# A ternary-expert transformer block on one core: the first block's attention worked by halves of its tokens, with its norms interleaved

## The chip, the core and the metric

The kernel runs on one core of one Trainium2 chip. The metric is the device time of one launch in microseconds (us). Below, PE is TensorE, DVE is VectorE, ACT is ScalarE, POOL is GpSimd and SP is the engine that issues the DMAs. PSUM is the memory that matmuls accumulate in.

## What is computed

4096 tokens of width 512 pass an attention over 64 fixed latent keys per head (16 heads of 32, the best four keys of each head count), and then a gated feed-forward layer whose three weight matrices are rounded to {-1, 0, 1} times one scale. Cut to what matters:

```python
Q = (h @ Wq.T + bq) by heads;  V = (h @ Wv.T + bv) by heads      # h = layernorm(x)
attn_logits = einsum('bhtd,lhd->bhtl', Q, latent) / sqrt(HD)
topk_logits, topk_idx = top_k(attn_logits, 4)
weighted = softmax(topk_logits) times the selected latents
x = x + layernorm((weighted + V) @ Wo.T + bo)
wu, wg, wd = ternary_quant(W_up), ternary_quant(W_gate), ternary_quant(W_down)
# ternary_quant(w): scale = mean(|w|) + 1e-8; clip(round(w / scale), -1, 1) * scale
g = layernorm(x)
x = x + layernorm((silu(g @ wu.T) * (g @ wg.T)) @ wd.T)
```

## The kernel before

The tokens are worked in eight blocks of 512, each of four tiles of 128 rows. A block's feed-forward layer is cut into 16 chunks of 128 hidden columns, called experts in the code. In the loop over the blocks (L687) the expert loop of block b carries the attention of block b+1 in pieces, placed by hand (`pieces`, L617: `put(e, k, f)` runs step f at place k of expert e). Only block 0's attention has no expert loop to hide in. It is written out ahead of the loop (L467 to L592), beside the preparation of the weights. The kernel uses a manual schedule: every engine carries out its instructions in the order in which the code issues them, and semaphores keep the data right.

The steps of an attention (class `Attention`, L211) are:

- `a_stats`, `a_rstd`, `a_apply`, `a_trans`: layer norm of a tile of x (statistics on DVE, the root on POOL in L190 and L191, the application on DVE) and its transposition by PE into `hT`, copied out of PSUM by ACT or DVE (L241, L243).
- `q(c)`: four matmuls of 128x512 into PSUM (L250), and ACT adds the bias (L255). c is one of four chunks of 128 columns, which hold four heads.
- `l(c)`: the logits of the chunk, in two PSUM tiles, one for each pair of heads, over all 512 tokens (L264); ACT scales them into two tiles w (L272). Such a pair is an "item" of 128 x 8 x 64 numbers, and there are eight items, i = 2c and 2c+1.
- `m(i)`, `r(i)`, `n(i)` on DVE: the eight largest of each row of 64 (L282), marking of the best four (L290), subtraction of the best (L292), and, after the exponentials `e(i)` on ACT (L299, L300), sum, reciprocal, mask and scaling (L305 to L310).
- `t(c)`: PE transposes two items (L322), ACT copies them to `wT` (L325). `v(c)`: the values, four matmuls (L334). `y(c)`: the weighted latents are added to the values in the same PSUM tile (L342), and ACT writes `attnT` with the bias (L346).
- `o(t, chunks)`: the output projection of token tile t (L355), accumulated over the four chunks. Before the loop, the four tiles' sums lie in four PSUM tiles (`acc_psum`) from the first chunk to the last.
- `o_bias`, `o_rstd`, `o_apply`: DVE adds the bias (L362) and takes statistics, POOL the root, DVE normalises (L196), and POOL or DVE adds to x (L371).
- `f_stats`, `f_rstd`, `f_apply`, `f_trans`: the second norm, the transposition (L206), and a split into two operands `hT_f` (ACT, L392) and `lT_f` (DVE, L393), which the experts' matmuls read.

An expert makes `pu` and `pg` (L409), DVE and ACT combine them to hidden columns, and `down` (L445) of the expert before adds its part to four PSUM tiles with the signs of the third matrix.

Each weight matrix (u, g, d) arrives in four chunks of 128x2048. `sum_abs` on ACT (L151, about 2 us) adds up the absolute values; `scale` adds the four sums over the partitions by a small matmul `tot` on PE (L155) and makes the scale and its inverse on DVE; `rounded` (L167, POOL, about 2 us) rounds a chunk, and `sign` (L171, ACT, about 2 us) makes the ternary chunk `tern`. The u and g chunks are prepared between the items of block 0's attention. Of d, two sums are taken at the end of that stage, and `down_weights` (L595) places the rest in the first experts: the two last sums and the scale in expert 0, the first sign in expert 1, the others in experts 2 to 4.

What limits the order around the change: `ps_at` holds two PSUM tiles that q, l, t, tot and all transpositions take in turn; `ps_up` holds two more (tags u and g), which v takes before the loop and pu and pg in it; `ps_acc` holds four.

Of the kernel before, what the change touches and what calls it, by code (L numbers as in the profile page):

```python
# [16 lines left out]
P = 128  # L17
# [15 lines left out]
def latent_attention_ternary_glu(  # L33
# [49 lines left out]
    x_tiles = {}  # L83

# [67 lines left out]

    def scale(n):
# [21 lines left out]
    class Norm:  # L175
        def __init__(self, name):
            self.name = name
            self.mv = small.tile([P, TT, 2], F32, tag="mv", name=f"mv_{name}")
            self.rs = small.tile([P, TT], F32, tag="rs", name=f"rs_{name}")

# [5 lines left out]
        def rstd(self, lo, hi, scale=None):  # L186
# [5 lines left out]
            if scale is not None:  # L192
                nc.gpsimd.tensor_scalar(rs, rs, scale[0], 0.0, ALU.mult, ALU.add)

# [16 lines left out]
    class Attention:  # L211
# [90 lines left out]
        def n(self, i):  # L302
            w = self.w[i]
            ri = small.tile([P, G], F32, tag="ri", name=f"ri_{self.b}_{i}")
# [92 lines left out]

    class Experts:
# [68 lines left out]
    A = Attention(0, hT_0, attnT_0)  # L467
# [4 lines left out]
    for t in range(TT):  # L472
        A.a_apply(t)
        A.a_trans(t, nc.vector if t % 2 else nc.scalar)
    nxt = Attention(1)

    def values(c):
        A.v(c, lambda name: ps_up.tile([P, 512], F32, tag="ug"[c % 2], name=name))

    def output(c):  # L480
        A.y(c)
        for t in range(TT):
            A.o(t, [c], acc_psum)

    sum_abs("u", 0)
# [3 lines left out]
    sum_abs("u", 2)  # L491
    A.q(1)

    A.m(0)
    A.r(0)
    A.e(0)

    sum_abs("u", 3)
    A.l(1)
    A.m(1)  # L500
    A.n(0)
    A.r(1)
    A.e(1)
# [4 lines left out]
    for k in range(DC):  # L508
        rounded("u", k, nc.gpsimd)

    A.q(2)
    values(0)
    sum_abs("g", 0)
    A.m(2)
    A.n(1)
    A.r(2)
    A.t(0)
    A.e(2)

    A.l(2)  # L520
    output(0)
    sum_abs("g", 1)
    A.m(3)
    A.n(2)
    A.r(3)
    A.e(3)

    A.q(3)
    values(1)
    sum_abs("g", 2)  # L530
    A.m(4)
    A.n(3)
    A.r(4)
    A.t(1)
    A.e(4)

    A.l(3)
    output(1)
    sum_abs("g", 3)
    A.m(5)  # L540
    A.n(4)
    A.r(5)
    A.e(5)
    scale("g")
    for k in range(DC):
        rounded("g", k, nc.gpsimd)

    values(2)
    sign("u", 0)
    A.m(6)  # L550
    A.n(5)
    A.r(6)
    A.t(2)
    A.e(6)

    output(2)
    values(3)
    sign("u", 1)
    sign("u", 2)
    A.m(7)  # L560
    A.n(6)
    A.r(7)
    A.e(7)

    sign("u", 3)
    A.n(7)
    A.t(3)
    output(3)
    for k in range(DC):
        sign("g", k)  # L570
    sum_abs("d", 0)
    sum_abs("d", 1)
    for t in range(TT):
        nxt.a_stats(t)
    nxt.a_rstd(0, 4)
    A.o_bias(0)
    A.o_bias(1)
    A.o_rstd(0, 2)
    A.o_bias(2)
    A.o_bias(3)  # L580
    A.o_rstd(2, 4)
    for t in range(TT):
# [209 lines left out]
```

## Time and profile before

| what | value |
|---|---|
| time before, median of 3 runs | 1259.86 us (1256.70 to 1261.38) |
| time of the profiled execution | 1260.48 us |
| its span in the profile | 1258.7 us |
| first value matmul (pv) of block 0 | 37.59 us |
| last output projection of block 0 begins | 84.84 us, for 3.70 us |
| last step n of block 0's items ends on DVE | about 80.4 us |
| HBM traffic over the span | 24.91 MB read, 8.39 MB written, 26 GB/s |

The page gives for each engine its busy time, then the busy share in 40 slices, then groups of instructions. Most of what matters here lies in the first three to four slices of 31.5 us each, so the page's averages say little of it; the busy time by stretch and the instructions in order of time do. In the latter, each row has start, duration, engine, line and operation, and in brackets how long the engine was idle before it and which instruction released it. "x8" for four f32 matmuls of q counts two passes of each. The DMA engines are busy from 2 to about 52 us with the weights and the first two blocks of x, and hardly at all afterwards:

```profile
25.00:40.00 15.00, 12.28 (x37) 5.82 (x36) 14.54 (x79) 7.65 (x13) 7.29 (x4) 0.77 1.02 404
40.00:55.00 15.00, 13.97 (x53) 6.82 (x52) 11.40 (x72) 8.48 (x15) 1.86 (x1) 1.00 0.88 323
55.00:70.00 15.00, 12.62 (x54) 6.31 (x52) 9.20 (x38) 8.99 (x15) 4.58 (x3) 1.00 0.00 1
```

The columns are the stretch and its length, then busy time and number of instructions of PE, weight load, DVE, ACT and POOL, then the granted TensorE clock as a share of full speed, the DMA share and GB/s.

### The profile page before, as it was taken

The numbers are of one execution on the slowest core, as the hardware profiler recorded it, in microseconds if no ns is written. First come the engines' busy times: TensorE is split into PE (matmuls) and PEld (weight loads), VectorE is DVE, ScalarE is ACT, GpSimd is POOL, SyncE is SP. The second block draws the span as 40 slices with busy tenths as digits, with TensorE's granted clock in tenths as the row PEclk, the third lists the DMA queues.
The fourth block names the chain that finished last, engine by engine and source line by source line (L and its number), as shares of the span: only waits on it lengthen the run. The fifth ranks groups of instructions, "written<-read, shape, count | busy, mean of one in ns | idle before, by whom it ended". The sixth has DMA issues, their size and how long they took to land.

```text
span 1258.7 us, 14275 instructions
## 1 busy us (share of the span) xinstructions
PE 1205.8 (96%) x4998; PEld 817.1 (65%) x4998; DVE 796.4 (63%) x2834; ACT 399.3 (32%) x675; POOL 174.2 (14%) x196
## 2 busy tenths in 40 slices
PE   5966999999999999999999999999999999999996
PEld 3424666676767666686675766666666767657884
DVE  4785575576747667485764767566684767737334
ACT  4574533133322333133331333213332233312221
POOL 0243000320003200032002210032000320013102
PEclk9996999999999999999999999999999999999998
DMA  9600000010000100001000010001000000000000
GB/s 366 260 1 0 1 1 1 0 36 33 1 1 1 68 1 1 1 1 67 1 1 1 1 68 1 1 1 67 1 2 0 1 35 1 1 1 1 34 1 34
DMA packets 14712, 34.21 MB, mean 27 GB/s; under 512 B 1456, under 2 KB 1456, under 8 KB 13616
## 3 DMA queue, kind: packets, MB, share of 16 engines
q1 hardware_dynamic: 14640, 33.30, 7.2%
q8 instruction: 39, 0.64, 0.2%
q14 instruction: 33, 0.27, 0.1%
HBM read 24.91 MB, written 8.39 MB: 26 GB/s over the span
## 4 chain that ended last, share of the span: by engine, by line
PE 89%; DVE 1%; POOL 1%; ACT 0%; issue 0%; POOLq 0%; ACTq 0%
PE pg L409 19%; PE acc L445 19%; PE pu L409 19%; PE pq L250 8%; PE po L355 8%; PE pv L334 8%; PE pv L342 2%; PE pw L322 2%; PE pl L264 2%; PE pt_f L206 1%; PE pt_a L206 1%; DVE h L426 0%; DVE y L196 0%; POOL x L460 0%; POOL rs_y L191 0%; ACT junk_high L151 0%
## 5 line engine op out<-in xcount | busy, mean ns | idle before, releaser
L409 PE MATMUL pg<-hT_f,tern_g 128*128 128x512 f32 x512 | 220.6, 431 | 0.0
L445 PE MATMUL acc<-tern_d,hi 128*128 128x512 f32 x512 | 213.5, 417 | 4.1 <-DVE y L196 4.1
L409 PE MATMUL pu<-hT_f,tern_u 128*128 128x512 f32 x512 | 210.2, 411 | 0.7 <-ACT hT_f L392 0.7
L426 DVE TENSOR_TENSOR h<-h,pg 128x512 f32<-128x512 f32 x128 | 87.3, 682 | 192.0 <-PE pg L409 191.2
L409 PE MATMUL pu<-lT_f,tern_u 128*128 128x512 f32 x512 | 204.0, 399 | 0.0
L409 PE MATMUL pg<-lT_f,tern_g 128*128 128x512 f32 x512 | 202.3, 395 | 0.0
L445 PE MATMUL acc<-tern_d,lo 128*128 128x512 f32 x512 | 202.1, 395 | 0.1
L418 ACT ACTIVATE h<-pu,half_u 128x512 f32<-128x512 f32 x128 | 87.7, 685 | 231.2 <-PE pu L409 230.1
L430 ACT CAST hi<-h 128x512 fp32r<-128x512 f32 x128 | 79.4, 621 | 253.9 <-DVE h L426 253.6
L421 DVE SCALAR_TENSOR_TENSOR h<-h,pu 128x512 f32<-128x512 f32 x128 | 87.0, 680 | 108.2 <-ACT h L418 108.2
L409 PEld LDWEIGHTS pg<-hT_f,tern_g 128*128 128x128 f32 x512 | 96.6, 189 | 51.4 <-issue 18.1
L250 PE MATMUL pq<-hT,wq 128*128 128x512 f32 x256 | 122.1, 622 | 1.5 <-issue 0.8
L445 PEld LDWEIGHTS acc<-tern_d,hi 128*128 128x128 f32 x512 | 96.4, 188 | 39.1 <-DVE y L196 12.2
L355 PE MATMUL po<-wo,attnT 128*128 128x512 f32 x256 | 115.5, 593 | 3.8 <-ACT attnT L346 3.8
L409 PEld LDWEIGHTS pg<-lT_f,tern_g 128*128 128x128 f32 x512 | 96.6, 189 | 28.5 <-issue 8.4
L334 PE MATMUL pv<-hT,wv 128*128 128x512 f32 x256 | 115.1, 592 | 0.0
L409 PEld LDWEIGHTS pu<-hT_f,tern_u 128*128 128x128 f32 x512 | 97.3, 190 | 24.1 <-issue 1.7
L409 PEld LDWEIGHTS pu<-lT_f,tern_u 128*128 128x128 f32 x512 | 97.3, 190 | 23.3 <-issue 1.7
L445 PEld LDWEIGHTS acc<-tern_d,lo 128*128 128x128 f32 x512 | 96.6, 189 | 22.8 <-issue 3.3
L435 DVE TENSOR_TENSOR lo<-h,hi 128x512 fp32r<-128x512 f32 x128 | 91.5, 715 | 21.9 <-ACT hi L430 21.9
L190 POOL TENSOR_SCALAR rs_o<-mv_o 128x2 f32<-128x2 f32 x16 | 5.7, 354 | 707.0 <-DVE mv_o L184 707.0
L290 DVE MATCH_REPLACE8 left<-m,w 128x64 f32<-128x64 f32 x512 | 100.4, 209 | 0.0
(101 smaller groups left out, 1336.1 us busy)
## 6 DMA issues: line engine op xcount, KB each, us to landing
x<-in_x SPq DMA_DIRECT2D x32, 256.0 KB, 4.0
out_x<-x SPq DMA_DIRECT2D x32, 256.0 KB, 2.0
raw_u<-in_wuT SPq DMA_DIRECT2D x4, 1024.0 KB, 11.8
raw_g<-in_wgT SPq DMA_DIRECT2D x4, 1024.0 KB, 16.6
raw_d<-in_wdT SPq DMA_DIRECT2D x4, 1024.0 KB, 16.2
wq<-in_wqT SPq DMA_DIRECT2D x1, 1024.0 KB, 7.5
wv<-in_wvT SPq DMA_DIRECT2D x1, 1024.0 KB, 16.7
wo<-in_woT SPq DMA_DIRECT2D x1, 1024.0 KB, 17.0
```

The costliest lines, as they stand in the source:

```text
L206: nc.tensor.transpose(pt[:, c * P : (c + 1) * P], h[:, c * P : (c + 1) * P], ident)
L250: nc.tensor.matmul(pq, lhsT=wq[:, k, c * P : (c + 1) * P], rhs=self.hT[:, k, :], start=(k == 0), stop=(k == DC - 1),)
L290: nc.vector.match_replace(left[:, g, :], m8[:, g, :], w[:, g, :], TAKEN)
L334: nc.tensor.matmul(self.pv[c], lhsT=wv[:, k, c * P : (c + 1) * P], rhs=self.hT[:, k, :], start=(k == 0), stop=False,)
L355: nc.tensor.matmul(self.po[t], lhsT=self.attnT[:, c, t * P : (t + 1) * P], rhs=wo[:, c, :], start=(c == 0), stop=(c == DC - 1),)
L409: nc.tensor.matmul(p, lhsT=tern[n][k][:, e * P : (e + 1) * P], rhs=part[:, k, :], start=(k == 0 and i == 0), stop=(k == DC - 1 and i == 1),)
L418: nc.scalar.activation(self.h[e], self.pu[e], AF.Tanh, scale=half_u[0])
L421: nc.vector.scalar_tensor_tensor(self.h[e], self.h[e], 1.0, self.pu.pop(e), ALU.add, ALU.mult)
L426: nc.vector.tensor_tensor(self.h[e], self.h[e], self.pg.pop(e), ALU.mult)
L430: nc.scalar.copy(hi, self.h[e])
L435: nc.vector.tensor_tensor(lo, self.h.pop(e), self.hid[e][0].bitcast(F32), ALU.subtract)
L445: nc.tensor.matmul(self.acc[t], lhsT=part[:, t * P : (t + 1) * P], rhs=wd, start=(e == 0 and i == 0), stop=(e == EC - 1 and i == 1),)
```

## The change

Block 0 gets a class of its own, `FirstAttention`. An item is now one chunk of four heads over one half of the tokens (256), instead of one pair of heads over all 512; item i is chunk i % 4 of half i // 4, and it is again 128 x 8 x 64 numbers, so m, r, e and n stay as they are. `l(c)` makes the items c and c+4, each through two PSUM tiles of which half is filled; items 4 to 7 lie in four buffers of the x tiles, which are free at that time. `t`, `v`, `y` and `o` go by item and work on 256 tokens. The bias of the output projection is put into PSUM by a matmul of one row (`o_begin`) ahead of the accumulation; the norm's statistics are taken from PSUM, and ACT applies it (`apply_scalar`, with a shift made by DVE). The order ahead of the loop is written anew: the norms of tiles 0 and 1 (o_stats to f_apply) stand between items 5 and 7, those of tiles 2 and 3 at the end. Two of the sums of u are taken by DVE. All four transpositions of the first norm are copied by ACT. The signs of g move to the end of the stage, the four sums of d into experts 0 and 1, the scale, the rounding and the first sign of d from expert 0 and the start of expert 1 to the middle of expert 1 ("high", just ahead of the first `down`). Of block 1's attention, `q(0)` moves from (1, 0) to (0, 2) and `q(1)` from (2, 0) to (1, 1).

In the two parts that write the order anew (-464 and -507), the removed lines are left out here (they are L464 to L592 above), and so are blank lines and some unchanged ones.

```diff
--- before.py
+++ after.py
@@ -81,6 +81,9 @@
     x_tiles = {}
+    w_later = [
+        work.tile([P, G, L], F32, tag="x", name=f"w_0_{4 + c}", bufs=3 * TT) for c in range(DC)
+    ]
     def load_x(b):
         x_tiles[b] = []
@@ -150,6 +153,11 @@
     def sum_abs(n, c, values=junk):
         nc.scalar.activation(values, raw[n][c], AF.Abs, accum_out=sums[n][:, c : c + 1])
+    def sum_abs_vector(n, c):
+        nc.vector.tensor_reduce(
+            sums[n][:, c : c + 1], raw[n][c], AX.X, ALU.add, apply_absolute_value=True
+        )
     def scale(n):
         tot = at_psum(f"tot_{n}")
         nc.tensor.matmul(tot[:, :DC], lhsT=ones, rhs=sums[n], start=True, stop=True)
@@ -177,6 +185,7 @@
             self.name = name
             self.mv = small.tile([P, TT, 2], F32, tag="mv", name=f"mv_{name}")
             self.rs = small.tile([P, TT], F32, tag="rs", name=f"rs_{name}")
+            self.nm = None
         def stats(self, t, src):
             st = small.tile([P, 6], F32, tag="st", name=f"st_{self.name}_{t}")
@@ -191,6 +200,20 @@
             nc.gpsimd.tensor_tensor(rs, rs, minus_half[:, : hi - lo], ALU.pow)
             if scale is not None:
                 nc.gpsimd.tensor_scalar(rs, rs, scale[0], 0.0, ALU.mult, ALU.add)
+        def shift(self, lo, hi):
+            if self.nm is None:
+                self.nm = small.tile([P, TT], F32, tag="nm", name=f"nm_{self.name}", bufs=1)
+            nc.vector.scalar_tensor_tensor(
+                self.nm[:, lo:hi], self.mv[:, lo:hi, 0], -1.0, self.rs[:, lo:hi],
+                ALU.mult, ALU.mult,
+            )
+        def apply_scalar(self, dst, src, t):
+            nc.scalar.activation(
+                dst, src, AF.Identity, bias=self.nm[:, t : t + 1], scale=self.rs[:, t : t + 1]
+            )
         def apply(self, dst, src, t):
             nc.vector.tensor_scalar(
@@ -301,7 +324,7 @@
         def n(self, i):
             w = self.w[i]
-            ri = small.tile([P, G], F32, tag="ri", name=f"ri_{self.b}_{i}")
+            ri = small.tile([P, G], F32, tag="ri", name=f"ri_{self.b}_{i}", bufs=2)
             nc.vector.tensor_reduce(ri, self.top.pop(i), AX.X, ALU.add)
             nc.vector.reciprocal(ri, ri)
             nc.vector.scalar_tensor_tensor(
@@ -395,6 +418,100 @@
             )
+    class FirstAttention(Attention):
+        HT = TB // 2
+        def l(self, c):
+            qT = self.qT.pop(c)
+            for th in range(2):
+                i = DC * th + c
+                if th == 0:
+                    self.w[i] = work.tile([P, G, L], F32, tag="w", name=f"w_0_{i}", bufs=4)
+                else:
+                    self.w[i] = w_later[c]
+                pls = [at_psum(f"pl_0_{i}_{pr}") for pr in range(2)]
+                for t in range(2):
+                    for pr in range(2):
+                        rows = slice(pr * HP, (pr + 1) * HP)
+                        tokens = slice((2 * th + t) * P, (2 * th + t + 1) * P)
+                        nc.tensor.matmul(
+                            pls[pr][:, t * P : (t + 1) * P],
+                            lhsT=qT[rows, tokens], rhs=lk[rows, c, :],
+                            start=True, stop=True, tile_position=(pr * HP, 0),
+                        )
+                for pr in range(2):
+                    nc.scalar.activation(
+                        self.w[i][:, pr * 4 : pr * 4 + 4, :],
+                        pls[pr][:, : self.HT].rearrange("p (g l) -> p g l", l=L), AF.Copy,
+                        scale=1.0 / math.sqrt(HD),
+                    )
+        def t(self, i):
+            w = self.w.pop(i)
+            self.wT[i] = work.tile([P, 2, TB], F32, tag="wT", name=f"wT_0_{i}", bufs=1)
+            pw = at_psum(f"pw_0_{i}")
+            for g in range(0, G, 2):
+                nc.tensor.transpose(pw[:, g * L : (g + 2) * L], w[:, g : g + 2, :], ident)
+            nc.scalar.copy(
+                self.wT[i][:, :, : self.HT], pw.rearrange("p (r k) -> p r k", k=self.HT)
+            )
+        def tokens(self, i):
+            return slice((i // DC) * self.HT, (i // DC + 1) * self.HT)
+        def v(self, i):
+            c = i % DC
+            self.pv[i] = ps_up.tile([P, TB], F32, tag="ug"[i % 2], name=f"pv_0_{i}")
+            for k in range(DC):
+                nc.tensor.matmul(
+                    self.pv[i][:, : self.HT], lhsT=wv[:, k, c * P : (c + 1) * P],
+                    rhs=self.hT[:, k, self.tokens(i)], start=(k == 0), stop=False,
+                )
+        def y(self, i):
+            c = i % DC
+            pv, wT = self.pv.pop(i), self.wT.pop(i)
+            for pr in range(2):
+                nc.tensor.matmul(
+                    pv[pr * HP : (pr + 1) * HP, : self.HT], lhsT=lv[:, 2 * c + pr, :],
+                    rhs=wT[:, pr, : self.HT], start=False, stop=True, tile_position=(0, pr * HP),
+                )
+            nc.scalar.activation(
+                self.attnT[:, c, self.tokens(i)], pv[:, : self.HT], AF.Identity,
+                bias=bqv_sb[:, 1, c : c + 1],
+            )
+        def o_begin(self, t):
+            self.po[t] = acc_psum(f"po_0_{t}")
+            nc.tensor.matmul(
+                self.po[t], lhsT=ones[0:1, :], rhs=bo_sb[0:1, :], start=True, stop=False
+            )
+        def o(self, i):
+            c = i % DC
+            for t in range(2 * (i // DC), 2 * (i // DC) + 2):
+                nc.tensor.matmul(
+                    self.po[t], lhsT=self.attnT[:, c, t * P : (t + 1) * P], rhs=wo[:, c, :],
+                    start=False, stop=(c == DC - 1),
+                )
+        def o_stats(self, t):
+            self.norm_o.stats(t, self.po[t])
+        def o_rstd(self, lo, hi):
+            self.norm_o.rstd(lo, hi)
+        def o_apply(self, t):
+            o = self.rows["o", t] = row(f"o_0_{t}")
+            self.norm_o.apply_scalar(o, self.po.pop(t), t)
+        def o_add(self, t):
+            nc.vector.tensor_tensor(self.x[t], self.x[t], self.rows.pop(("o", t)), ALU.add)
     class Experts:
         def __init__(self, b, parts):
             self.b = b
@@ -464,42 +581,36 @@
...
+    A = FirstAttention(0, hT_0, attnT_0)
     for t in range(TT):
         A.a_stats(t)
             A.a_rstd(t - 1, t + 1)
     for t in range(TT):
         A.a_apply(t)
+    for t in range(TT):
+        A.a_trans(t)
+    sum_abs_vector("u", 0)
     sum_abs("u", 1)
     A.q(0)
     A.l(0)
+    sum_abs_vector("u", 2)
     A.q(1)
+    sum_abs("u", 3)
     A.m(0)
     A.r(0)
+    A.l(1)
     A.e(0)
+    A.q(2)
     A.m(1)
     A.n(0)
     A.r(1)
+    A.l(2)
     A.e(1)
     scale("u")
@@ -507,96 +618,132 @@
...
     for k in range(DC):
         rounded("u", k, nc.gpsimd)
+    A.q(3)
     A.m(2)
     A.n(1)
     A.r(2)
+    A.l(3)
+    A.v(0)
     A.t(0)
     A.e(2)
+    sum_abs("g", 0)
+    A.y(0)
     A.m(3)
     A.n(2)
     A.r(3)
+    A.v(1)
+    A.t(1)
+    A.y(1)
     A.e(3)
+    sum_abs("g", 1)
+    for t in range(2):
+        A.o_begin(t)
+    A.o(0)
+    A.v(2)
+    A.t(2)
+    A.y(2)
+    A.o(1)
     A.m(4)
     A.n(3)
+    A.v(3)
+    A.t(3)
     A.r(4)
+    A.y(3)
     A.e(4)
+    sum_abs("g", 2)
+    sign("u", 0)
+    A.o(2)
+    A.o(3)
     A.m(5)
     A.n(4)
     A.r(5)
+    A.v(4)
+    A.t(4)
     A.e(5)
+    A.y(4)
+    sum_abs("g", 3)
+    sign("u", 1)
+    for t in range(2):
+        A.o_stats(t)
+    A.o_rstd(0, 2)
+    for t in range(2, 4):
+        A.o_begin(t)
+    A.o(4)
+    A.m(6)
+    A.n(5)
+    A.norm_o.shift(0, 2)
+    A.o_apply(0)
+    A.o_apply(1)
+    A.r(6)
+    A.v(5)
+    A.t(5)
+    A.y(5)
+    A.e(6)
+    sign("u", 2)
     scale("g")
     for k in range(DC):
         rounded("g", k, nc.gpsimd)
+    A.o(5)
+    for t in range(2):
+        A.o_add(t)
+        A.f_stats(t)
+    A.f_rstd(0, 2)
     A.m(7)
     A.n(6)
+    A.v(6)
+    A.t(6)
     A.r(7)
+    A.y(6)
     A.e(7)
     sign("u", 3)
+    A.o(6)
+    A.v(7)
+    for t in range(2):
+        A.f_apply(t)
     A.n(7)
+    A.t(7)
+    A.y(7)
+    A.o(7)
+    sign("g", 0)
+    A.f_alloc()
+    nxt.a_stats(0)
+    nxt.a_stats(1)
+    for t in range(2):
+        A.f_trans(t)
+    for t in range(2, 4):
+        A.o_stats(t)
+        A.o_rstd(t, t + 1)
+    sign("g", 1)
+    nxt.a_stats(2)
+    for t in range(2, 4):
+        A.norm_o.shift(t, t + 1)
+        A.o_apply(t)
+    for t in range(2, 4):
+        A.o_add(t)
+        A.f_stats(t)
+        A.f_rstd(t, t + 1)
+    sign("g", 2)
+    nxt.a_stats(3)
+    for t in range(2, 4):
         A.f_apply(t)
+    for t in range(2, 4):
         A.f_trans(t)
+    sign("g", 3)
     def down_weights(e, place):
+        if (e, place) in ((0, "tanh"), (0, "high"), (0, "down"), (1, "tanh")):
+            c = ((0, "tanh"), (0, "high"), (0, "down"), (1, "tanh")).index((e, place))
+            sum_abs("d", c, work.tile([P, CH], BF16, tag="wT", name=f"junk_d_{c}", bufs=1))
+        elif (e, place) == (1, "high"):
             scale("d")
@@ -606,7 +753,6 @@
             out_scale.extend((first, square))
             for k in range(DC):
                 rounded("d", k, nc.gpsimd)
-        elif (e, place) == (1, "up"):
             sign("d", 0)
         elif e in (2, 3, 4) and place == "gate":
             sign("d", e - 1)
@@ -629,9 +775,10 @@
         put(0, 1, A.a_apply, 3)
         put(0, 2, A.a_trans, 2)
         put(0, 2, A.a_trans, 3)
-        put(1, 0, A.q, 0)
+        put(*((0, 2) if A.b == 1 else (1, 0)), A.q, 0)
         put(1, 1, A.l, 0)
-        put(2, 0, A.q, 1)
+        put(*((1, 1) if A.b == 1 else (2, 0)), A.q, 1)
         put(2, 2, A.l, 1)
         put(3, 0, A.q, 2)
         put(4, 0, A.q, 3)
```

More of the change, by code (lines that the diff above doesn't have):

```diff
@@ L466, in latent_attention_ternary_glu @@
     out_scale = []
-    A = Attention(0, hT_0, attnT_0)
+    A = FirstAttention(0, hT_0, attnT_0)
     for t in range(TT):
@@ L473, in latent_attention_ternary_glu @@
         A.a_apply(t)
-        A.a_trans(t, nc.vector if t % 2 else nc.scalar)
+    for t in range(TT):
+        A.a_trans(t)
     nxt = Attention(1)
[L477 to L487, printed above, removed]
+    sum_abs_vector("u", 0)
     sum_abs("u", 1)
@@ L490, in latent_attention_ternary_glu @@
     A.l(0)
-    sum_abs("u", 2)
+    sum_abs_vector("u", 2)
     A.q(1)
+    sum_abs("u", 3)
     A.m(0)
     A.r(0)
+    A.l(1)
     A.e(0)
-    sum_abs("u", 3)
-    A.l(1)
+    A.q(2)
     A.m(1)
@@ L509, in latent_attention_ternary_glu @@
         rounded("u", k, nc.gpsimd)
-    A.q(2)
-    values(0)
-    sum_abs("g", 0)
+    A.q(3)
     A.m(2)
@@ L516, in latent_attention_ternary_glu @@
     A.r(2)
+    A.l(3)
+    A.v(0)
     A.t(0)
     A.e(2)
-    A.l(2)
-    output(0)
-    sum_abs("g", 1)
+    sum_abs("g", 0)
+    A.y(0)
     A.m(3)
@@ L525, in latent_attention_ternary_glu @@
     A.r(3)
+    A.v(1)
+    A.t(1)
+    A.y(1)
     A.e(3)
-    A.q(3)
-    values(1)
-    sum_abs("g", 2)
+    sum_abs("g", 1)
[6 more added lines that the diff above has]
+    A.o(1)
     A.m(4)
     A.n(3)
+    A.v(3)
+    A.t(3)
     A.r(4)
-    A.t(1)
+    A.y(3)
     A.e(4)
-    A.l(3)
-    output(1)
-    sum_abs("g", 3)
+    sum_abs("g", 2)
+    sign("u", 0)
+    A.o(2)
+    A.o(3)
     A.m(5)
@@ L546, in latent_attention_ternary_glu @@
         rounded("g", k, nc.gpsimd)
[L548 to L559, printed above, removed]
+    A.o(5)
[3 more added lines that the diff above has]
+    A.f_rstd(0, 2)
     A.m(7)
     A.n(6)
+    A.v(6)
+    A.t(6)
     A.r(7)
+    A.y(6)
     A.e(7)
     sign("u", 3)
+    A.o(6)
+    A.v(7)
+    for t in range(2):
+        A.f_apply(t)
     A.n(7)
[L567 to L574, printed above, removed]
-    nxt.a_rstd(0, 4)
[L576 to L582, printed above, removed]
-        A.o_apply(t, nc.vector if t % 2 else nc.gpsimd)
-    for t in range(TT):
-        A.f_stats(t)
-        if t % 2:
-            A.f_rstd(t - 1, t + 1)
-    A.f_alloc()
-    for t in range(TT):
+    A.t(7)
[21 more added lines that the diff above has]
+    nxt.a_stats(3)
+    nxt.a_rstd(0, 4)
+    for t in range(2, 4):
         A.f_apply(t)
-    for t in range(TT):
+    for t in range(2, 4):
         A.f_trans(t)
+    sign("g", 3)
     def down_weights(e, place):
-        if (e, place) in ((0, "tanh"), (0, "high")):
-            values = work.tile([P, CH], BF16, tag="wT", name=f"junk_{place}", bufs=1)
-            sum_abs("d", 2 + (place == "high"), values)
-        elif (e, place) == (0, "down"):
+        if (e, place) in ((0, "tanh"), (0, "high"), (0, "down"), (1, "tanh")):
+            c = ((0, "tanh"), (0, "high"), (0, "down"), (1, "tanh")).index((e, place))
+            sum_abs("d", c, work.tile([P, CH], BF16, tag="wT", name=f"junk_d_{c}", bufs=1))
+        elif (e, place) == (1, "high"):
             scale("d")
```

## The prediction

> **What bounds the kernel now.** I read the page's busy shares and slices first, then the busy time by stretch, then the queues of the first 130 us in order of time.
>
> ```profile
> PE 1205.8 (96%) x4998; PEld 817.1 (65%) x4998; DVE 796.4 (63%) x2834; ACT 399.3 (32%) x675; POOL 174.2 (14%) x196
> ...
> PE   5966999999999999999999999999999999999996
> ```
>
> TensorE is full from slice 5 to slice 39. What changes ahead of that shifts everything behind it; gains there need an earlier start or fewer gaps.
>
> ```profile
> 70.00:85.00 15.00, 12.13 (x37) 5.23 (x38) 12.82 (x62) 10.42 (x13) 5.75 (x4) 1.00 0.01 1
> 85.00:100.00 15.00, 3.54 (x8) 1.28 (x8) 13.55 (x25) 11.58 (x8) 5.83 (x9) 0.72 0.00 1
> 100.00:115.00 15.00, 12.28 (x46) 9.42 (x47) 8.29 (x16) 6.29 (x10) 1.31 (x3) 0.60 0.00 0
> 115.00:130.00 15.00, 12.76 (x55) 8.38 (x54) 4.83 (x9) 7.94 (x11) 8.27 (x4) 0.89 0.00 1
> 130.00:145.00 15.00, 15.00 (x64) 9.64 (x63) 8.79 (x45) 6.31 (x9) 0.00 (x0) 1.00 0.00 0
> ```
>
> The columns are PE, weight load, DVE, ACT, POOL, granted clock, DMA. From 85 to 100 us DVE works through the norms of four tiles while PE does 3.5 of 15 us; afterwards PE runs at a reduced clock. From 130 us on PE has no gap.
>
> ```profile
> 31.18 6.57 PE L250 MATMUL pq<-hT,wq 128*128 128x512 f32 x8
> ...
> 84.84 3.70 PE L355 MATMUL po<-wo,attnT 128*128 128x512 f32 x8 [0.78 <-ACT attnT L346]
> 101.14 1.94 PE L206 MATMUL pt_f<-ident,h_f 128*128 128x128 f32 x8 [12.59 <-DVE h_f L196]
> ...
> 106.34 0.79 PE L409 MATMUL pu<-hT_f,tern_u 128*128 128x512 f32 x1 [0.68 <-ACT hT_f L392]
> ...
> 117.65 0.38 PE L155 MATMUL tot_d<-sums_d,ones 128*128 128x4 f32 x2 [2.24 <-ACT hT L243]
> ...
> 127.94 0.50 PE L445 MATMUL acc<-tern_d,hi 128*128 128x512 f32 x1
> ```
>
> Two marks follow: S, the first expert matmul (pu), at 106.34; and the end of the first down product at 129.89 (the next pu starts there), S+23.55. The down product waits for nothing, since tern_d_0 is made in 125.68 to 127.68 on ACT, from a rounding that began at 118.78 on POOL.
>
> **What the Trainium skill says.** "TensorE: Matmul & The Clock Gate", Part 1: an idle PE falls to half rate and a window of about 3.4 us decides. The trace agrees: clock 0.50 from 31 to 37 us, and the same four-matmul q takes 6.57 us there and 3.43 to 3.70 warm. "GPSIMD Engine Reference", Key points: GpSimd shares SBUF interfaces with VectorE, against instructions with two SBUF inputs. The trace agrees:
>
> ```profile
> 35.27 2.35 DVE L310 TENSOR_TENSOR w<-w,ri 128x512 f32<-128x512 f32 x1
> ...
> 44.14 0.69 DVE L310 TENSOR_TENSOR w<-w,ri 128x512 f32<-128x512 f32 x1
> ```
>
> The first lies beside the rounding, the second does not; a whole step n takes 3.85 instead of 1.58 us, r only 2.48 instead of 2.39. "Perfetto Trace Analysis", Tensor Engine Instruction: ACT and DVE are strictly in order, PE only pulls weight loads ahead. Agrees: pu of expert 1 stood behind the waiting tot_d at 117.65. "VectorE: DVE Perf Modes", tier table: tensor_reduce has only the 1x rate; 2048 elements at that page's 0.96 GHz are an estimated 2.1 us, which no row here shows.
>
> DVE's two longest waits between items, which other work could fill:
>
> ```profile
> 58.01 0.19 DVE L305 TENSOR_REDUCE ri<-top 128x8 f32<-128x32 f32 x1 [4.40 <-ACT top L299]
> ...
> 64.71 0.16 DVE L157 TENSOR_REDUCE total_g<-tot_g 128x1 f32<-128x4 f32 x1 [2.31 <-PE tot_g L155]
> ```
>
> **Unit costs, from the queues in order of time.** DVE per item: m 1.18, n 1.58, r 2.39. PE warm: a 128x512 f32 matmul 0.86, so v on 256 tokens 1.72 and one o item (two matmuls) 1.72; four transposes 0.52; y half of 1.08. ACT: sum_abs 2.02, sign 2.07, wT, attnT and w about 0.4 to 0.6, the exp pair 0.65. Work that halves its tokens I price by half plus the fixed part.
>
> **The change before S, walked queue by queue (us).**
> - Start. All four hT copies go to ACT and DVE's h_a is no longer behind copies: hT complete at 12.4 against 13.8. q0 12.4 to 19.1 (cold, 6.68). The two DVE sums (4.3 together) lie in DVE's old wait of 9.39 before the first MAX8: cost nothing; if that cover failed, m0 would start up to 2 later.
> - Items. A pair item came two to a q; now each q gives one early item and one for the second half, so the first four items need all four q. Each l also fills and empties the two PSUM buffers twice, and the next q waits for that: w_0 at 21.3, q1 22.35 to 26.05; on ACT the sum of raw_u_3 (2.02) stands ahead of w_1, so w_1 only at 29.5. q2 30.45 to 37.0 if cold as at 31.18, q3 40.55 to 44.2, pl_7 done 46.9.
> - DVE meanwhile: m0 21.3, r0 done 25.0, waits for w_1 until 29.5; n0, r1 done 35.1; then total_u waits until 40.55, because tot_u stands on PE behind q2 and both pl of chunk 2. Behind that wait stand m2 and n1, and POOL's rounding of u. n1 costs 3.85; r2 done 48.6, r3 54.15, m5 60.5.
> - From 46.9 PE is its own bound. Per item v 1.72, t 0.52, wait for wT 0.65, y 0.54, o 1.72; plus four new bias matmuls of 0.86. That puts t(3) at 64.8, e(4) at 67.0 (ACT has wT_3 and attnT_3 ahead of it), so DVE waits 6.5 from 60.5. v(6) ends at 83.8.
> - tot_g (79.8) now sits behind y(5). DVE then has scale (0.5), two adds to x beside POOL's rounding of g (2.35 each as in the row above; 0.69 if uncovered), two f_stats (0.8 each), m7 (1.2) and n6 (about 2.4, partly beside rounding): done 90.4. PE idles 83.8 to 90.4 and goes cold.
> - The tail. t6, y6, o6, v7, t7, y7, o7 with their ACT hops, part cold: 12.3, to 102.7. First half's f_trans and lT_f 2.5 (105.2): DVE has these ahead of the second half's o_stats. Then o_stats x2 1.6, POOL's second rstd 1.1 (0.19+0.71 and hops), shift 0.15, the two ACT applies to 109.1, add and f_stats one after the other to 111.4, rstd 1.0, f_apply 0.8, transpose cold 1.5, copy 0.7: S = 115.4.
> The old tail, from the end of n7 (80.35) to S, was 26.0. The first half's norms do leave it (two o_bias and o_stats 3.1, add and apply 2.6, f_stats 1.6, f_apply 0.5: 7.8), but o is not finished sooner: po was complete at 88.5 before, and is at 102.7 now.
> Bounds: the new q0 starts 1.4 earlier in the clock's windows, so q2 may be warm (-3.1, and -1.1 from q0); adds uncovered -3.3; late stretch warm -2. Low end 115.4-9.5 = 105.9, so -0.4; high end +2 for hops I left out, +11. The likeliest takes half the clock's 4.2: S = 113.3, **+7.0**.
>
> **The change after S.** q of block 1, chunk 0, moves ahead of expert 1's pu, into the old wait for hT; q0 cannot start before hT_3 (S+11.8) and pu_1 not before q0. Ends: S+18.8 against S+18.65, no gain. ACT now has all four d sums there (two stood at 92.87 to 96.8, in the old tail), so w_0 comes at S+22.85; q1, pulled forward, waits 1.05 for it (two PSUM buffers) and ends S+26.35. Then tot_d, scale 0.5, one rounding 2.07, one sign 2.0 lie between tot_d and the first down product, which needs tern_d_0: it starts at S+31.25, ends S+33.1. PE stands still 4.65; nothing may pass it. Without the moved q1 (3.43) that is 29.7 against 23.55: +6.1. A pause over one window leaves PE at half rate once more, as at 119 us, where 3.4 us of work took double: +1.7 (between 0 and +3). Together **+7.8** (6 to 9). Later experts: rounding of d runs ahead of their signs; no cost. SP's order of DMAs is unchanged; w_later takes x buffers that block 2's loads need only at expert 4, long after t(7). The DVE accumulations that o_bias made are on PE, the applies on ACT, both counted above.
>
> Sum: 1258.7 + 7.0 + 7.8 = 1273.5 span; the profiled run is 1.8 above its span and 0.6 above the median: 1273.5 + 1.2 = **1274.7**.
>
> **Rivals.**
> 1. The tail's saving meets the new wait and they cancel: items end at 80 as before, S = 106.3-7.8 = 98.5, after S +7.8: 1260. For it: 12.59 us of PE idle stands there to be taken. Against: po complete 14 us later in my walk.
> 2. Ends on the other side: DVE's item chain closes up, its waits (4.40, 2.31 and smaller) filled by norm work. Bound by DVE: 21.3 + 8x5.15 + 11.5 (two scales 1, norms 5.9, contention 4.6) = 74, tail 20 as I walk it: S = 94, so -12.3; after S +6: 1253.5. It decides once items end before about 74.5, which needs total_u, e(4) and tot_g without waits; PE's 39.7 us of work after 46.9 speaks against.
> 3. Slower still: every cold stretch happens and hops add up: +11 +9, 1280.
>
> **Chances.** Forecast with its bounds (1266 to 1278) 0.66, rival 3 0.18, rival 1 0.09, rival 2 0.07. A measurement of this kernel can tell about 0.5% (6.3 us) from no change. Faster 0.07, same 0.09, slower 0.84. The range 1264 to 1282 leaves out rival 2, most of rival 1 and the end of rival 3.
>
> **What would show it.** Right: pu's first matmul at 109 to 116; DVE waiting for PE tot_u about 5 us and for exp of item 4 about 6; PE waiting for DVE before t(6); the first acc waiting 4 to 5 us for ACT's tern_d. Wrong: pu before 104, or no wait at the first acc.

## The result, and the profile after

The changed kernel takes 1279.03 us (median of 4 runs, 1278.40 to 1280.23), the kernel before 1259.16 us (4 runs, 1256.70 to 1261.38). The ratio is 1.0174, with a 95% interval of 1.0156 to 1.0191: slower by 1.7%. The profiled execution took 1280.23 us, with a span of 1278.5 us, 19.8 more than before (1258.7).

The busy shares and slices of the changed kernel:

```profile
PE 1213.8 (95%) x5054; PEld 825.9 (65%) x5054; DVE 796.1 (62%) x2831; ACT 400.0 (31%) x689; POOL 172.3 (13%) x198
...
PE   5866799999999999999999999999999999999996
```

TensorE is full from slice 6 on, one slice later than before. The loss lies ahead of that, so the stretches from 85 to 130 us come next (same columns as before: length, PE, weight load, DVE, ACT, POOL, clock, DMA share, GB/s):

```profile
85.00:100.00 15.00, 7.27 (x22) 3.72 (x21) 14.07 (x45) 4.54 (x6) 9.14 (x6) 0.66 0.06 17
100.00:115.00 15.00, 6.19 (x30) 3.76 (x28) 7.15 (x17) 9.26 (x9) 2.37 (x6) 0.84 0.06 17
115.00:130.00 15.00, 10.12 (x40) 7.63 (x40) 7.26 (x15) 9.50 (x13) 2.40 (x5) 0.70 0.00 1
```

Before, one stretch of 15 us was poor in PE work (85 to 100). Now there are two (85 to 115), and the one from 115 to 130 has 10.1 us of PE where it had 12.8. From 85 to 100 DVE is busy for 14.07 us and POOL for 9.14: they work side by side, while PE waits. The marks on PE, in order of time:

```profile
55.78 3.58 PE L496 MATMUL po<-wo,attnT 128*128 128x512 f32 x4
...
80.93 0.60 PE L456 MATMUL pw<-ident,w 128*128 128x128 f32 x4
...
85.31 1.89 PE L468 MATMUL pv<-hT,wv 128*128 128x256 f32 x8
93.63 1.08 PE L456 MATMUL pw<-ident,w 128*128 128x128 f32 x4 [6.43 <-DVE w L333]
...
104.64 1.98 PE L496 MATMUL po<-wo,attnT 128*128 128x512 f32 x4 [0.57 <-ACT attnT L481]
106.46 1.04 PE L229 MATMUL pt_f<-ident,h_f 128*128 128x128 f32 x8
116.83 1.94 PE L229 MATMUL pt_f<-ident,h_f 128*128 128x128 f32 x8 [9.34 <-DVE h_f L219]
119.45 0.79 PE L526 MATMUL pu<-hT_f,tern_u 128*128 128x512 f32 x1 [0.68 <-ACT hT_f L415]
...
150.24 0.79 PE L562 MATMUL acc<-tern_d,hi 128*128 128x512 f32 x1 [4.81 <-ACT tern_d L179]
```

S, the first expert matmul, stands at 119.45 instead of 106.34 (+13.1). The wait of 12.59 us ahead of the norm's transposes is only 9.34 long now, but a new one of 6.43 stands before item 6's transposes, and the last output projection ends 18 us later than before (106.5 against 88.5). The row at 80.93 is item 5's transposes, from which the experiments below measure. Behind S the down product waits 4.81 us for the first sign of d. By the spans the part behind S costs 19.8 - 13.1 = 6.7 us.

What PE waits for at 93.63 is on DVE. Its queue ahead of that:

```profile
68.79 0.22 ACT L322 ACTIVATE top<-top 128x32 f32<-128x32 f32 x1
```

```profile
69.04 0.18 DVE L328 TENSOR_REDUCE ri<-top 128x8 f32<-128x32 f32 x1 [8.79 <-ACT top L322]
...
83.27 0.16 DVE L165 TENSOR_REDUCE total_g<-tot_g 128x1 f32<-128x4 f32 x1 [3.09 <-PE tot_g L163]
...
83.73 0.67 DVE L512 TENSOR_TENSOR x<-x,o 128x512 f32<-128x512 f32 x1
...
85.27 1.51 DVE L512 TENSOR_TENSOR x<-x,o 128x512 f32<-128x512 f32 x1
...
89.10 2.00 DVE L330 SCALAR_TENSOR_TENSOR w<-left,w 128x512 f32<-128x512 f32 x1
91.14 2.34 DVE L333 TENSOR_TENSOR w<-w,ri 128x512 f32<-128x512 f32 x1
```

```profile
83.97 8.97 POOL L175 TENSOR_SCALAR raw_g<-raw_g,inv_g 128x2048 f32<-128x2048 f32 x4 [7.94 <-ACT top L322]
```

The first fence is ScalarE's exponential of item 4, the second DVE, the third POOL. DVE waits 8.79 us for the exponential and 3.09 for `tot_g`. POOL's rounding of g runs from 83.97 to 92.94, and from the second add on every DVE pass with two tensor inputs beside it is long: 1.51, 2.00 and 2.34 us, where a pass of the same size takes 0.67 to 0.69 alone.

### The profile page after: what moved, and what is told of

It is laid out like the page before. It is cut to its first block, busy times and chain, and to the rows that moved or that the text cites. A ratio compares the mean times of both kernels' runs of the same rounds, so it can differ in the third digit from the quotient of the medians.

```text
span 1278.5 us, 14396 instructions
## 1 busy us (share of the span) xinstructions
PE 1213.8 (95%) x5054; PEld 825.9 (65%) x5054; DVE 796.1 (62%) x2831; ACT 400.0 (31%) x689; POOL 172.3 (13%) x198
## 4 chain that ended last, share of the span: by engine, by line
PE 91%; issue 3%; DVE 2%; ACT 1%; DMA 1%; POOL 1%; SPq 0%; POOLq 0%; ACTq 0%
PE acc L562 19%; PE pg L526 19%; PE pu L526 18%; PE pq L273 8%; PE po L378 8%; PE pv L357 8%; PE pv L365 2%; PE pw L345 2%; PE pl L287 2%; PE po L496 1%; PE pt_f L229 1%; PE pv L468 1%; PE pt_a L229 1%; DMA raw_u<-in_wuT 1%; PE pl L439 1%
## 5 line engine op out<-in xcount | busy, mean ns | idle before, releaser
L199 POOL TENSOR_SCALAR rs_o<-mv_o 128x2 f32<-128x2 f32 (+1 forms) x17 | 5.6, 332 | 735.1 <-DVE mv_o L193 735.0
L378 PE MATMUL po<-wo,attnT 128*128 128x512 f32 x224 | 100.7, 592 | 0.0
L357 PE MATMUL pv<-hT,wv 128*128 128x512 f32 x224 | 100.6, 592 | 0.0
## 6 DMA issues: line engine op xcount, KB each, us to landing
raw_d<-in_wdT SPq DMA_DIRECT2D x4, 1024.0 KB, 16.5
```

Of the source, the lines that this page charges most:

```text
L357: nc.tensor.matmul(self.pv[c], lhsT=wv[:, k, c * P : (c + 1) * P], rhs=self.hT[:, k, :], start=(k == 0), stop=False,)
L378: nc.tensor.matmul(self.po[t], lhsT=self.attnT[:, c, t * P : (t + 1) * P], rhs=wo[:, c, :], start=(c == 0), stop=(c == DC - 1),)
```

## The experiments

The theory after the result had two parts. First, the d part behind S costs about 7 us. Second, the 13 us ahead of S come from DVE's and PE's order in the halves. Each row below is one kernel, some with several edits. The ratios are to the kernel before on the same chip; the medians come from different rounds, so the ratios are what to compare. "S" is the start of the first expert matmul and "after S" the profiled span less S, which shows the d part in one view:

| kernel | median us (runs) | ratio to before, 95% interval | S | after S |
|---|---|---|---|---|
| before | 1259.16 (4) | | 106.34 | 1152.4 |
| changed | 1279.03 (4) | 1.0174 [1.0156, 1.0191] | 119.45 | 1159.1 |
| before, d part of the change | 1264.86 (6) | 1.0059 [1.0038, 1.0079] | 105.09 | 1159.9 |
| changed, d sums early | 1268.51 (4) | 1.0096 [1.0062, 1.0131] | 116.14 | 1148.5 |
| changed, bias by ident | 1277.44 (4) | 1.0160 [1.0132, 1.0187] | 115.39 | 1159.3 |
| changed, scale of u early | 1279.52 (4) | 1.0175 [1.0151, 1.0198] | 118.35 | 1159.1 |
| changed, two v in the q stretch | 1280.51 (4) | 1.0187 [1.0170, 1.0205] | 118.88 | 1159.0 |
| changed, items 6 and 7 first | 1279.41 (4) | 1.0178 [1.0155, 1.0201] | 118.08 | 1158.7 |
| changed, four repairs | 1269.07 (4) | 1.0094 [1.0074, 1.0113] | 119.66 | 1148.8 |
| the same, rounding of g last | 1259.09 (22) | 1.0014 [1.0005, 1.0024] | 111.20 | 1147.9 |
| changed, rounding of g last | 1272.17 (6) | 1.0105 [1.0086, 1.0125] | 110.70 | 1160.4 |
| changed, rounding of g last, d sums early | 1260.34 (22) | 1.0024 [1.0013, 1.0034] | 106.76 | 1149.2 |
| before, four d sums in the tail | 1252.73 (10) | 0.9970 [0.9954, 0.9985] | 104.67 | 1148.8 |
| before, parts without halves | 1248.34 (5) | 0.9932 [0.9916, 0.9949] | 99.67 | 1146.9 |

S comes from one profiled execution of each kernel, and it also moves with where PE's half clock falls in that execution. The changed kernel and the one with only the rounding of g last are the same program up to item 5, yet the first value matmul of their profiles starts at 46.38 and at 44.31. So what an edit behind item 5 does ahead of S is read below from item 5's transposes on.

### The d part: alone, and taken back

Before, with only this (and q of block 1 moved as in the change):

```diff
-    sum_abs("d", 0)
-    sum_abs("d", 1)
...
-        if (e, place) in ((0, "tanh"), (0, "high")):
+        if (e, place) in ((0, "tanh"), (0, "high"), (0, "down"), (1, "tanh")):
...
-        elif (e, place) == (0, "down"):
+        elif (e, place) == (1, "high"):
             scale("d")
```

> The kernel before, with only the part of the change that lies after S: the four sums of d in experts 0 and 1, scale, rounding and first sign of d in the middle of expert 1, and the two moved q. My theory (the chain tot_d, scale, rounding, sign ahead of the first down product is a cost of its own, independent of the attention stage): S stays within 1 us of 106.3, the first acc waits 4 to 5 us for ACT's tern_d, and the time is 6 to 8 us above the kernel before (about 1266). Rival (the wait only arises because the changed attention leaves ACT late): no wait, within 2 us of the kernel before.

And the changed kernel, with the sums behind `sign("u", 2)` and scale, rounding and first sign of d where they stood before:

```diff
     sign("u", 2)
+    for c in range(DC):
+        sum_abs("d", c)
...
+        if (e, place) == (0, "down"):
             scale("d")
```

> The changed kernel, with the four sums of d in the stretch of about 8.8 us in which ACT waits for pw of item 6, and scale, rounding and first sign of d where the kernel before has them. My theory: the wait of 4.8 us at the first acc goes, the copies of hT in expert 0 are no longer behind sums of d, S moves by less than 1 us: 7 to 10 us below the changed kernel (1269 to 1272), still 10 to 13 above the kernel before, which is the attention stage's share. Rival (the two parts share a cause, the late ACT): under 4 us below.

Measured: the first run is 0.59% slower than the kernel before and has the same wait, shown here from its list of PE's waits (line, what it waits for, us in total, times, longest). The second is 0.8% faster than the changed kernel by the ratios and has no such wait.

```profile
PE acc L445 <- ACT tern_d L171: 4.8, 1, 4.8
```

The column "after S" says it most clearly: all seven kernels with late sums have 1158.7 to 1160.4, the six with early sums 1146.9 to 1149.2, and the kernel before, with two early and two late, 1152.4. The late d part costs about 7 us against before, and 10 to 11 against sums that are all early. The second figure is larger since before still sums two chunks of d in expert 0. The moved q has no visible part in it: the changed kernel with early sums keeps the move and has 1148.5, the kernel before with all four sums in its tail doesn't have it and has 1148.8. In the second run S came 3.3 us earlier, where under 1 was expected. That lies ahead of its edit: item 5's transposes start at 77.41 instead of 80.93, and from there to S it takes 38.73 us instead of 38.52.

### Three edits ahead of S that brought nothing

The output bias by a full 128-row operand, for the change's one-row matmul:

```diff
-                self.po[t], lhsT=ones[0:1, :], rhs=bo_sb[0:1, :], start=True, stop=False
+                self.po[t], lhsT=ident, rhs=bo_sb, start=True, stop=False
```

> The changed kernel, with the bias of the output projection brought into PSUM by the identity (128 rows) times the bias already copied to all partitions, in place of a product of one row. Same number of matmuls and columns. Theory A (one-row matmuls do not count as activity for the clock gate, so the clock halves from 55.8 to 59.2 us): the clock stays at 1.00 there, o of item 0 takes 1.9 instead of 3.58 us, S 1.5 to 2 us earlier, time about 1277.3. Theory B (the clock halves because of the waits for wT before it): no change of the clock, time within 0.5 us.

The profiled execution had no half clock at the first output projection (o took 1.88 us, not 3.58) and S at 115.39. But the median is 1277.44, and the interval of its ratio overlaps that of the changed kernel. Of the 4.1 us by which S is earlier, 2.5 stand ahead of the first bias matmul, where the two programs are the same (first value matmul at 43.93 instead of 46.38). The same one-row matmuls ran without a half clock after them in the profile with early d sums, and in the run with four repairs the two ident matmuls themselves ran at half clock (3.78 us for 1.98). So whether one row matters is not settled.

The scale and rounding of u ahead of q(2), so that DVE doesn't wait for `tot_u`:

```diff
     A.m(1)
-    A.n(0)
-    A.r(1)
-    A.l(2)
-    A.e(1)
     scale("u")
...
+    A.q(2)
+    A.n(0)
```

> The changed kernel, with tot_u and the scale of u ahead of q(2), so that DVE no longer waits 4.36 us for tot_u at 35.6. My theory (from 46 to 88 us PE's order is what ends last, and DVE has 8.8 us of waiting left at item 4): S moves by less than 1.5 us, time within 1.5 us of the changed kernel. Rival (DVE's chain of items is what bounds the stage): 3 to 4.4 us below the changed kernel.

DVE's wait went from 4.36 us to 0.4, and the time stayed: 1279.52. The wait of 8.8 for the exponential of item 4, further on, still ended when PE and ACT let it. What DVE gained ahead of it went into waiting: 2.88 us for an earlier exponential, where it had been 0.41.

The values of items 0 and 1 in the q stretch, to shorten PE's queue behind it:

```diff
     A.r(0)
+    A.v(0)
     A.l(1)
...
-    A.v(0)
     A.t(0)
```

> The changed kernel, with v of items 0 and 1 moved forward into PE's idle places while it waits for q's evacuations (after q(1) and after q(2)). My theory (PE's order from 46 us on bounds the attention stage): two v of 1.7 us leave the bound stretch, S 2.5 to 5 us earlier, time 2.5 to 5 us below the changed kernel. Rival (DVE's chain bounds it): S within 1 us.

The expectation of 2.5 to 5 us was missed. The first transposes of w came at 44.95 instead of 48.22, but PE then stood at half clock and gave it back (same rows as above):

```profile
51.17 3.78 PE L489 MATMUL po<-bo_sb,ones 1*128 1x512 f32 x4
54.88 3.78 PE L496 MATMUL po<-wo,attnT 128*128 128x512 f32 x4
...
65.70 0.60 PE L456 MATMUL pw<-ident,w 128*128 128x128 f32 x4
```

Item 3's transposes, at 66.38 in the changed kernel, start at 65.70: of 3.3 us, 0.7 are left.

### Where DVE meets POOL

Items 6 and 7 ahead of the adds, scale and rounding of g behind these:

```diff
-    scale("g")
-    for k in range(DC):
-        rounded("g", k, nc.gpsimd)
     A.o(5)
+    A.m(7)
+    A.n(6)
+    A.v(6)
+    A.t(6)
     for t in range(2):
         A.o_add(t)
         A.f_stats(t)
     A.f_rstd(0, 2)
...
+    scale("g")
+    for k in range(DC):
+        rounded("g", k, nc.gpsimd)
```

> The changed kernel, with m(7) and n(6) ahead of the two adds, the second norm's statistics and the scale of g on DVE, and rounding of g behind them. My theory (the wait of 6.43 us for n(6), half of it DVE queueing ahead of n(6), half of it POOL's rounding beside n(6), is a cost on the path): the wait before pw of item 6 goes to under 1 us, t(7) is 4 to 6 us earlier, S and the time 3.5 to 6 us below the changed kernel. Rival (what is put behind n(6) comes back before t(7) or in the tail): under 1.5 us.

The rival of the expectation was right. The wait before item 6 was gone, and one of 6.36 us stood before item 7. On DVE in that stretch:

```profile
88.88 1.56 DVE L315 TENSOR_TENSOR w<-w,m 128x512 f32<-128x512 f32 x1
90.36 0.18 DVE L317 TENSOR_TENSOR top<-m 128x32 f32<-128x32 f32 x1
90.47 4.23 DVE L219 TENSOR_SCALAR h_f<-x,mv_f,rs_f 128x512 f32<-128x512 f32 x2
...
94.94 2.12 DVE L330 SCALAR_TENSOR_TENSOR w<-left,w 128x512 f32<-128x512 f32 x1
```

The rounding (87.93 to 96.5 here) had only moved on to other work: 1.56 us instead of 0.69, 4.23 instead of 1.00 and 2.12 instead of 0.69. That is 5.5 us more than alone, which is most of the wait. All four repairs together (d sums in ScalarE's idle places, bias by ident, two v moved, this order) had the same contention:

> The changed kernel with the repairs together: early d (its sums in ACT's idle places, scale and first sign as in the kernel before), bias by the identity, v of items 0 and 1 hoisted, n(6) first. If the costs add: 10 (d) + 3.5 + 5 + 1.7 = 20 us below the changed kernel, so within 4 us of the kernel before; S at 103 to 109. If they share slack: 5 or more above the kernel before.

1269.07 is what the d part alone gives back (1268.51); S was 119.66. So the next run moved only the rounding of g of that kernel, behind n(7), and two more did the same to the changed kernel itself, without and with early d sums (the edit as it stands against the changed kernel):

```diff
-    scale("g")
-    for k in range(DC):
-        rounded("g", k, nc.gpsimd)
...
     A.n(7)
+    scale("g")
+    for k in range(DC):
+        rounded("g", k, nc.gpsimd)
     A.t(7)
```

> The kernel with all repairs (sums of d early, output bias by ident and bo_sb, values of items 0 and 1 in the q stretch, items 6 and 7 ahead of the adds), and scale and rounding of g now behind n(7). That kernel stood at 1269.1 us, its first expert matmul at 119.7, with PE waiting 6 us for item 7's weights. Theory A, POOL's rounding of g beside VectorE makes that wait (f_apply 4.23 for two instead of 1.0, n(7) and r(7) 2.3 each): t(7) comes 4 to 6 us earlier, the first expert matmul at 113 to 116, time 1263 to 1266. Rival: the wait only moves on, since the rounding of g now stands ahead of the signs of g and these or the second layer norm are late, or the half clock eats it: the first expert matmul at 118 or later, time 1267.5 to 1270.

> The changed kernel with one edit: scale and rounding of g (8 to 9 us of POOL, in the changed kernel ahead of the adds and items 6 and 7) now behind n(7). Theory A, this one placement is most of the front's loss, because every VectorE pass of items 6 and 7 beside it takes two to four times as long: PE's wait of 6.4 us before item 6's transposes gone and none in its place, the first expert matmul at 110 to 113 instead of 119.5, the 4.8 us before the first down product unchanged, time 1269 to 1272, 7 to 10 below the changed kernel. Rival B, it counts only together with the values in the q stretch, the bias by ident and items 6 and 7 ahead of the adds: the first expert matmul at 116 or later, time 1275 or more.

> The changed kernel with two edits: scale and rounding of g behind n(7), and the sums of d early, in ScalarE's idle places, with scale, rounding and first sign of d where they stood in the kernel before. Theory A, these two are the whole loss that can be taken back in this order: time 1258 to 1262, within 3 us of the kernel with all repairs (1259.1) and level with the kernel before. Rival B, the output bias by ident, the values in the q stretch or items 6 and 7 ahead of the adds carry part of that kernel's gain: time 1264 or more.

All three went the way of theory A in their expectations: the rounding makes the wait. The first went further than that theory said (1263 to 1266): 1269.07 became 1259.09, the ratio 1.0094 became 1.0014. The changed kernel's ratio fell from 1.0174 to 1.0105, and with early d sums too to 1.0024. One placement of one POOL step is worth about 9 to 10 us (8.7 and 10.1 by the ratios of the two pairs that differ in it alone), and bias, v and items together about 1 (1.0014 against 1.0024, intervals that overlap).

The time from item 5's transposes to S leaves out the half clock's luck ahead of them. It is 38.5 to 39.0 us in the changed kernel and in the four runs that leave the rounding where it was, 38.9 with items 6 and 7 first and 39.5 with the four repairs. With the rounding last it is 30.15, 30.15 and 31.14. In both pairs the move gives 8.4 us. In the changed kernel 6.6 of them lie between item 5's and item 6's transposes, where PE waits for DVE, and 2.2 between item 6's and item 7's, where PE works at half clock behind that wait (the output projection between them took 3.38 us, 1.99 with the rounding last); behind item 7, 0.4 is given back. So the second part of the theory holds only for the place of the rounding; the edits of the order that left POOL beside DVE brought nothing. What then remains of the 13.1 us ahead of S is 4.4 in one of the changed kernel's two profiles with the rounding last (110.70) and 0.4 in the other (106.76). That is within what the half clock moves, and its cause is left open.

The changed kernel with only this edit, on DVE and then on PE:

```profile
78.38 0.66 DVE L512 TENSOR_TENSOR x<-x,o 128x512 f32<-128x512 f32 x1
...
83.72 0.69 DVE L330 SCALAR_TENSOR_TENSOR w<-left,w 128x512 f32<-128x512 f32 x1
84.45 0.69 DVE L333 TENSOR_TENSOR w<-w,ri 128x512 f32<-128x512 f32 x1
```

```profile
80.55 0.60 PE L456 MATMUL pw<-ident,w 128*128 128x128 f32 x4
...
86.66 0.60 PE L456 MATMUL pw<-ident,w 128*128 128x128 f32 x4
...
92.90 0.63 PE L456 MATMUL pw<-ident,w 128*128 128x128 f32 x4
...
95.49 1.98 PE L496 MATMUL po<-wo,attnT 128*128 128x512 f32 x4 [0.57 <-ACT attnT L481]
```

None of these passes is long, and PE's transposes wait for no w. The rounding lies at 93.79 to 101.61 now, where DVE has little else. The edit takes away two things at once, the contention (1.51, 2.00 and 2.34 less 0.67, 0.69 and 0.69: 3.8 us) and DVE's wait of 3.09 for `tot_g` with the 0.5 of the scale, 7.4 in all. The two weren't measured apart in this place. But in the kernel with four repairs DVE did not wait for `tot_g`, so the 8.4 us that the move brought there is contention (1.57, 4.24 and 2.13 us less 0.69, 1.00 and 0.69: 5.6), the 0.5 of the scale, and PE's half clock behind the wait.

### What is worth keeping

The kernel before, with all four sums of d in its tail, and then with those parts of the change that need no halves: the sums of d in ScalarE's idle places, the bias on PE by ident, the norm's application on ScalarE, two signs of g behind the tail (and `ri` in two buffers, as in the change). The sums of g also move one place earlier, and the norms' last steps go by pairs of tiles.

> The kernel before, with all four sums of d in the tail, where ACT waits from 97 to 102 us. Theory (the copies of hT in expert 0 stand behind sums of d on ACT, which costs PE 2.24 us and a cold stretch of some 3.4 us at half rate): both go, time 3 to 4 us below the kernel before. Rival (PE only waits at the next place): within 1 us.

```diff
-            A.o(t, [c], acc_psum)
+            A.o(t, c)
...
+    for t in range(TT):
+        A.o_begin(t)
...
+    sum_abs("d", 0)
...
-        A.o_apply(t, nc.vector if t % 2 else nc.gpsimd)
+    A.norm_o.shift(0, 2)
+    A.o_apply(0)
+    A.o_apply(1)
+    for t in range(2):
+        A.o_add(t)
```

> The kernel before with the order by pairs of heads kept, and only those parts of the change that need no halves: all four sums of d in ScalarE's idle places of the first attention, the output bias added on TensorE, the norm's application on ScalarE, two signs of g behind the tail. Theory A, the change's parts are good and its order by halves is what costs: the first expert matmul at 100 to 103 (106.3 before), nothing added after it, time 1246 to 1252, 0.5 to 1% faster than before and 2 to 6 us below the kernel with the four sums of d in the tail. Rival, the parts themselves cost: the four more sums delay q, the exponentials and the sign of u on ScalarE, which is then the bound of the front: first expert matmul at 105 or later, time 1254 to 1262.

Both are faster than the kernel before: 0.3% and 0.68% (interval 0.5 to 0.84%), 1248.34 us. The tail of the second on PE:

```profile
82.27 3.70 PE L419 MATMUL po<-wo,attnT 128*128 128x512 f32 x8 [0.78 <-ACT attnT L361]
94.47 1.94 PE L221 MATMUL pt_f<-ident,h_f 128*128 128x128 f32 x8 [8.50 <-DVE h_f L211]
...
99.67 0.79 PE L445 MATMUL pu<-hT_f,tern_u 128*128 128x512 f32 x1 [0.67 <-ACT hT_f L407]
```

From the end of the last output projection to S it takes 99.67 - 85.97 = 13.7 us, 17.8 before. In the changed kernel it is 119.45 - 106.46 = 13.0, with the rounding of g moved 13.0 to 13.4. So the tail by halves is hardly shorter than that of four tiles with the same parts, while the projection ends later: at 93.4 in the best profile by halves, 86.0 here. Against the two kernels by halves with the rounding last and early d sums (1.0014 and 1.0024) the kernel without halves (0.9932) is 10 to 12 us faster by the ratios. This run is several edits at once, and its parts are not all those of the others, so it compares whole kernels and prices neither each part nor the order alone.

## Why the prediction was right or wrong

It was right in sign and near in size: 1274.7 forecast, 1279.03 measured, within the stated 1264 to 1282. It is less right than that sounds. The time lies above the forecast's own bounds (1266 to 1278) and 1 us under rival 3 (1280). The bound of 1278 was also narrower than its two upper ends together, 1258.7 + 11 + 9 + 1.2 = 1279.9. And S left its own bounds: +13.1, where -0.4 to +11 was told, and 119.45, where the sign of being right was 109 to 116. The waits that were to show it all came: 4.36 us for `tot_u` (about 5 told), 8.8 for the exponential of item 4 (about 6), PE's wait before item 6's transposes, and 4.81 at the first down product (4 to 5).

The difference of 4.3 us is 6.1 too little ahead of S, 1.1 too much behind it, and 0.7 too much between span and median. It lies in these terms.

- **After S**, forecast +7.8, measured +6.7 by subtraction and +7.5 in the run with the d part alone (1159.9 - 1152.4). The chain was as told: PE stood 4.81 (4.65 told), the moved q waited 0.79 for w (1.05), the first down product came at S+30.8 (S+31.25) and took 3.6 us at half clock, 1.95 before (+1.7 told).
- **Before S**, forecast +7.0, measured +13.1: 6.1 short, of which 2.1 is the step "the likeliest takes half the clock's 4.2" and 4.05 the walk itself (115.4 against 119.45). Of the clock's gain 0.75 came (q3 at 39.80 for 40.55) and was lost again: q0 was warm (3.70 us), but its copy to `qT` then stood behind the sum of raw_u_1 on ScalarE (15.31 to 17.22). Here the profile matters: in the run with only the rounding of g moved, the same program up to item 5, q3 came at 37.74.
- The walk, "from 46.9 PE is its own bound": it was, from 46.38. From there to t(3) the walk had 17.9 us and the trace 20.0, since the first output projection ran at half clock (3.58 us for 1.72); from t(3) to `tot_g` 15.0 against 16.5, in part since the period of an item (from transposes to transposes) is 5.46 (60.92 to 66.38) where the sum had 5.15. So the exponential of item 4 came at 68.8 instead of 67.0 (DVE waited 8.8, not 6.5) and `tot_g` at 82.84 instead of 79.8: 3.0 of the 4.05.
- From `tot_g` to the end of n6 the walk had 10.6 us, and the trace has 10.6 (82.84 to 93.48), by two errors that cancel: the adds were priced 2.35 each and took 0.67 and 1.51, n6 was priced 2.4, partly beside the rounding, and took 4.7, almost wholly beside it. So PE's wait before item 6's transposes, 6.43 us where the walk had 6.6, is right in its cause and by luck in its size. Which pass meets the rounding has to be walked in time, not by the order of the lines.
- From there to the end of the projection 13.0 (12.3 told), to S another 13.0 (12.7): the last 1.0 of the 4.05.
- DVE's wait for total_u was right in place and size and, as the run without it shows, it cost nothing. That fits the walk, which has PE as the bound from 46.9 on.
- DVE's two sums of u, an estimate of 2.1 us each, took 2.29 (`TENSOR_REDUCE`), in the old wait, as told.
- Rival 2, the order by halves as a gain, failed as argued: PE's own work behind the q stretch sets the items. Rival 1's saved tail (7.8) was real only as 17.8 - 13.0 = 4.8, and the same parts give 4.1 of it without halves.

What the prediction lacked is the weight of one line: it priced the adds beside the rounding as a bound of 3.3 us and did not ask what moving the rounding would do, though this was the largest single cost ahead of S (8.4 us from item 5 to S).

## What to carry to other kernels

Place a long GpSimd step by what VectorE has in those microseconds. Beside it, a pass took two to four times its time here, and a rounding of 8 to 9 us, put in a stretch where VectorE was the next thing TensorE waited for, cost 9 to 10 us. A tail that is shortened by interleaving must be compared with the tail after the cheap repairs (work moved to idle engines); here these gave 4.1 of the 4.8 us without any interleaving. And a sum that is put off comes back at its first reader: taking the sums of d ahead of S, where ScalarE was idle, was worth 10 us of 1280 against taking them behind it.

## What the runs showed of the hardware

- A pass of one SBUF input and two scalars on DVE suffered most beside POOL's rounding: `f_apply` of two 128x512 tiles took 4.23 us beside it and 1.00 alone, while 128x512 passes of two inputs went from 0.69 to between 1.5 and 2.35. The Trainium skill, "GPSIMD Engine Reference", Key points, names two kinds of VectorE instructions that collide with GpSimd, those in a 2-port mode and those with two SBUF inputs. The second kind agrees with these runs; whether `f_apply` ran in such a mode no run shows. The sizes are from these runs. POOL's own rounding of four chunks took 7.82 us with little beside it and 8.97 beside the adds and n6.
- The half clock falls in other places from one profile to the next, in the same order of work. The changed kernel, the run with items 6 and 7 first and the one with only the rounding moved are the same program up to item 5. Their first three q took 3.70, 5.50 and 5.40 us in the first profile, 5.64, 3.70 and 5.40 in the second, and 6.22, 3.70 and 3.70 in the third. With only the rounding moved, bias, o and v at 71.8 to 80.7 took 2.63, 3.78 and 2.83 us, and 1.98, 1.98 and 1.89 with the d sums early too. The Trainium skill, "TensorE: Matmul & The Clock Gate", Part 1, says that the window is free-running; these runs fit that, and a forecast for this kernel could not count on a warm or cold stretch of 3 us.
